# A factorization-machine kernel: four embeddings at a time, 512 moving columns in every product, outer products in two passes of 128 rows, sums in place

## The chip, the core and the metric

The kernel runs on one core of a Trainium2 chip. The metric is device time in microseconds (us), the median of several runs. The core's engines each run a queue of their own, in order: TensorE (PE; its weight loads are shown as PEld), VectorE (DVE), ScalarE (ACT), GpSimd (POOL) and SyncE (SP), which only issues transfers here. Transfers that POOL issues can add to what lies at their destination; transfers that SP issues copy. All of them share 16 DMA engines.

## The reference

```python
out_lin = x @ lin_w.T + lin_b                               # x (1024, 512)
xv = jnp.einsum('bf,efm->bem', x, weight)                   # weight (64, 512, 512)
zp = jnp.einsum('bf,efm->bem', jnp.square(x), jnp.square(weight))
interaction = 0.5 * jnp.sum(jnp.square(xv) - zp, axis=1)
return out_lin + interaction
```

All is float32. For each of 64 embeddings e, x is multiplied by a 512 x 512 matrix, the result is squared, and the squares are summed over e. The sum of zp over e is one product, x squared times the sum of the squared matrices, and is done once at the end.

## The kernel before

The products are made by a two-level block algorithm that needs seven products in place of eight at each level (numbered 1 to 7 at both). The outer level splits the rows of x in two (r), the features in two (kk), and the right side by embedding: a step q takes two embeddings (v), so its four weight blocks are (kk, v). The inner level splits each of those products in the same way. The seven by seven sums of x blocks are kept in `xs`; the sums of weight blocks are made anew for each q by POOL: `outer_t` (L341) makes the outer sums 5, 6, 7 and 4 as tiles `to`, 1,024 elements a partition, and `inner_t` (L373) makes the inner sums 5, 7, 6 and 4 of each outer operand as a tile `ti` (three operations through `sums_t`, L361). `ti` and `to` have three buffers each, the weights four, `z` (results) six, `w2` two.

`block_product` (L403) does one outer product: seven inner products, each by `product` (L389), which multiplies two row halves j of 128 rows by the same 256 moving columns, into the two halves of one PSUM bank. A product in float32 is two instructions on TensorE. Three PSUM tags, x, v and y, hold the partial results: ACT copies x to y after product 1 (L457), then 6, 7 and 4 are added into y, so product 6 waits for ACT's copy. DVE takes results out, with the outer level's sums (`SUMS`, L518): z1, z2, z3, z4, z5 and the four result blocks c11, c12, z5 (which becomes the third) and c21. For outer product 7 POOL adds a part (L446).

`squares` (L476) has ACT square a result block of 2,048 elements a partition in place, and POOL issue one accumulating transfer of 1 MB that adds it to `acc[0]` or `acc[1]`. `w_squares` (L497) squares a weight matrix into a `w2` tile and adds that to `w2_sum` in the same way. A transfer into the same accumulator waits, on POOL, until the one before has landed.

The order is written out by hand: `st.at(t, fn)` gives each piece of work a place t in a stream, and `Stream.run` (L23) emits everything sorted by t. One unit of t is one product (four instructions) in the main loop. Outer products start 7 apart and overlap: at times 0, 2, 4, 6 stand products 1, 5, 6, 2 of one, and between them 7, 3, 4 of the one before. So a step q of two embeddings is 49 units, and there are 32. The stream time fixes only the order in each queue; waits between engines do the rest. SP loads the weights of step q at 49q - 48.8 in transfers of 1 MB.

After the loop the last product (L625 to L749) uses `w2_sum` and the squares of x, and joins the accumulators and the linear part; that linear part is computed at the start (L185 to L300).

Of the kernel before, what the change touches and what calls it, by code (L numbers as in the profile page):

```python
# [28 lines left out]
def kernel(  # L29
# [29 lines left out]

    nc = tc.nc  # L60
# [8 lines left out]
    wpool = ctx.enter_context(tc.tile_pool(name="wpool", bufs=4))  # L69
    topool = ctx.enter_context(tc.tile_pool(name="topool", bufs=3))  # L70
    tipool = ctx.enter_context(tc.tile_pool(name="tipool", bufs=3))
    w2pool = ctx.enter_context(tc.tile_pool(name="w2pool", bufs=2))
    spool = ctx.enter_context(tc.tile_pool(name="spool", bufs=3))
    zpool = ctx.enter_context(tc.tile_pool(name="zpool", bufs=6))
# [7 lines left out]
    w2_sum = const.tile([P, NK, M], F32, tag="w2_sum", name="w2_sum")  # L82
    acc = [
        const.tile([P, 4, BK], F32, tag=f"acc{r}", name=f"acc{r}") for r in range(2)
    ]

# [7 lines left out]
    raw_sb = zpool.tile([P, 7, Q], F32, tag="z", name="raw_sb")  # L94
    a21_sb = w2pool.tile([P, 4, Q], F32, tag="w2", name="a21_sb")
    lw_sb = wpool.tile([P, NK, M], F32, tag="w", name="lw_sb")
# [74 lines left out]
    A21_SUMS = zpool.tile([P, 4, Q], F32, tag="z", name="A21_sums")  # L171
    lt_sb = zpool.tile([P, 2, 4, HM], F32, tag="z", name="lt_sb")
    LT = [lt_sb[:, kk] for kk in range(2)]
# [31 lines left out]
    def lin_out(n):  # L205
        s, j = n // 2, n % 2
        nc.scalar.activation(
            acc[0][:, 2 * s : 2 * s + 2, ts(j, HM)],
            LIN[n].rearrange("p (u c) -> p u c", u=2),
            AF.Copy,  # L210
            scale=2.0,
        )
# [28 lines left out]
    def lin_p(o, bank, first):  # L241
        def fn():
            if o == "1":
                for n in "xvy":
                    LIN[n] = psum.tile(
                        [P, BK], F32, tag=n, name=f"{n}_lin", bufs=2 if n == "x" else 3
                    )
                for n in ("s5", "s2"):
                    LIN[n] = spool.tile([P, BK], F32, tag=n, name=f"{n}_lin")
            for kk in range(2):  # L250
                for j in range(2):
                    nc.tensor.matmul(  # L252
                        LIN[bank][:, ts(j, HM)],
                        lin_x(kk, o)[:, ts(j, P)],
                        operand_b(lw_sb[:, ts(kk, 2)], LT[kk], o),
                        start=(first and kk == 0 and j == 0),
                        stop=True,
                        skip_group_check=True,
                    )

        return fn

    def twice(bank, dst):
        def fn():
            o = LIN[dst] if dst in ("s5", "s2") else acc[1][:, dst]
            nc.scalar.activation(o, LIN[bank], AF.Copy, scale=2.0)
# [3 lines left out]
    def lin_join(bank, s, blk):  # L270
        def fn():
            nc.vector.scalar_tensor_tensor(
                acc[1][:, blk], LIN[bank], 2.0, LIN[s], ALU.mult, ALU.add
# [5 lines left out]
    for kk in range(2):  # L279
        st.at(-30 + 8 * kk, lambda kk=kk: lin(kk))  # L280
        st.at(-30 + kk, lambda kk=kk: sums_t(LT[kk], lw_sb[:, ts(kk, 2)]))
# [22 lines left out]
    def add_bias(r, b):  # L304
        o = acc[r][:, b].rearrange("p (j c) -> p j c", j=2)
        nc.vector.scalar_tensor_tensor(
            o,
            bias[:, ts(b % 2, HM)].unsqueeze(1).broadcast_to([P, 2, HM]),
            2.0,
            o,  # L310
            ALU.mult,
            ALU.add,
        )

    st.at(-1, lambda: nc.sync.dma_start(bias, lin_b.partition_broadcast(P)))


    for b in range(4):
        for r, t in enumerate((23.6, 25.6)):
            st.at(49 * (b + 1) + t, lambda r=r, b=b: add_bias(r, b))  # L320

    W = {}

    def load_w(q):
        for v in range(2):
            W[q, v] = wpool.tile([P, NK, M], F32, tag="w", name=f"w{q}_{v}")
        src = [weight[2 * q + v].rearrange("(p k) m -> p k m", k=NK) for v in range(2)]
        if q == 0:
            for kk in range(2):
                for v in range(2):  # L330
                    nc.sync.dma_start(W[q, v][:, ts(kk, 2)], src[v][:, ts(kk, 2)])
        else:
            for v in range(2):
                nc.sync.dma_start(W[q, v], src[v])

    def w_block(q, kk, v):
        return W[q, v][:, 2 * kk : 2 * kk + 2, :]

    TO = {}

    def outer_t(q, i):  # L341
        B11, B12 = w_block(q, 0, 0), w_block(q, 0, 1)
        B21, B22 = w_block(q, 1, 0), w_block(q, 1, 1)
        t = topool.tile([P, 2, M], F32, tag="to", name=f"to{q}_{i}")
        TO[q, i] = t
        a, b = {
            "5": lambda: (B12, B11),
            "6": lambda: (B22, TO[q, "5"]),
            "7": lambda: (B22, B12),
            "4": lambda: (B21, TO[q, "6"]),  # L350
        }[i]()
        nc.gpsimd.tensor_sub(t, a, b)  # L352

    def outer_b(q, i):
        if i in "123":
            return w_block(q, *{"1": (0, 0), "2": (1, 0), "3": (1, 1)}[i])
        return TO[q, i]
# [3 lines left out]
    def sums_t(t, b):  # L361

        nc.gpsimd.tensor_sub(  # L363
            t[:, 0:2, :],
            b[:, :, HM:M],
            b.rearrange("p l m -> p (l m)")[:, 0:M].rearrange(
                "p (u c) -> p u c", u=2
            ),
        )
        nc.gpsimd.tensor_sub(t[:, 2, :], b[:, 1, HM:M], t[:, 0, :])  # L370
        nc.gpsimd.tensor_sub(t[:, 3, :], b[:, 1, 0:HM], t[:, 2, :])

    def inner_t(q, i):  # L373
        TI[q, i] = tipool.tile([P, 4, HM], F32, tag="ti", name=f"ti{q}_{i}")
        sums_t(TI[q, i], outer_b(q, i))

    def operand_b(b, t, o):
        return {
            "1": lambda: b[:, 0, 0:HM],
            "2": lambda: b[:, 1, 0:HM],  # L380
            "3": lambda: b[:, 1, HM:M],
            "5": lambda: t[:, 0, :],
            "7": lambda: t[:, 1, :],
            "6": lambda: t[:, 2, :],
            "4": lambda: t[:, 3, :],
        }[o]()


    def product(ps, q, i, o, start):  # L389
        rhs = operand_b(outer_b(q, i), TI[q, i], o)  # L390
        for j in range(2):
            nc.tensor.matmul(  # L392
                ps[:, ts(j, HM)],
                xsl(i, o)[:, ts(j, P)],
                rhs,
                start=(start and j == 0),
                stop=True,
                skip_group_check=True,
            )

    Z = {}

    def block_product(t0, q, i, sums):  # L403
# [3 lines left out]
        (addend, name), *more = sums  # L407
        d = {}

        def p(o, bank, start):  # L410
            def fn():
                product(d[bank], q, i, o, start)
# [3 lines left out]
        def p1():  # L416
            for n in "xvy":
                d[n] = psum.tile(
                    [P, BK], F32, tag=n, name=f"{n}{q}_{i}", bufs=2 if n == "x" else 3
                )  # L420
            for n in ("s5", "s2"):
                d[n] = spool.tile([P, BK], F32, tag=n, name=f"{n}_{q}_{i}")
            for n in (name, *(m[1] for m in more)):
                if (q, n) not in Z:
                    Z[q, n] = zpool.tile([P, 4, BK], F32, tag="z", name=f"z{q}_{n}")
            p("1", "x", True)()

        def out_of(bank, dst, blk):
            def fn():
                if addend is None and dst is not None:  # L430
                    nc.scalar.copy(d[dst], d[bank])
                elif addend is None and not more:
                    nc.scalar.copy(Z[q, name][:, blk], d[bank])
                elif addend is not None:
                    o = Z[q, name][:, blk] if dst is None else d[dst]
                    nc.vector.tensor_add(o, d[bank], Z[q, addend][:, blk])  # L436
                for a, n, _ in more if dst is None else ():
                    nc.vector.tensor_add(Z[q, n][:, blk], d[bank], Z[q, a][:, blk])
# [3 lines left out]
        def rest(engine, blk):  # L442
            def fn():
                for _, n, by in more:
                    z = [Z[q, m][:, blk] for m in (n, name, by)]
                    engine.tensor_add(*z)  # L446
# [3 lines left out]
        def join(bank, s, blk):  # L450
            def fn():
                nc.vector.tensor_add(Z[q, name][:, blk], d[bank], d[s])  # L452

            return fn

# [3 lines left out]
        st.at(t0 + 2.5, out_of("v", "s5", 3))  # L459
        st.at(t0 + 4, p("6", "y", False))  # L460
        st.at(t0 + 4.5, out_of("y", "s2", 1))
        st.at(t0 + 6, p("2", "x", False))
        st.at(t0 + 6.5, out_of("x", None, 0))
        st.at(t0 + 8, p("7", "y", False))
        st.at(t0 + 8.5, join("y", "s5", 3))
        st.at(t0 + 10, p("3", "v", False))
        st.at(t0 + 10.5, join("v", "s2", 1))
        st.at(t0 + 12, p("4", "y", False))
        st.at(t0 + 12.5, out_of("y", None, 2))
        if i == "5":  # L470
            st.at(t0 + 9.6, rest(nc.vector, 3))
            st.at(t0 + 11.6, rest(nc.vector, 1))
        elif more:
            st.at(t0 + 11.6, rest(nc.gpsimd, slice(1, 4, 2)))

    def squares(t, q, name, r, wait=5):  # L476
        def sq():
            z = Z[q, name]
# [304 lines left out]
```

## Time and profile before

| | |
|---|---|
| median of 3 runs | 1414.64 us (1413.63 to 1414.66) |
| the profiled execution: device time | 1414.79 us |
| the profiled execution: span, first to last instruction | 1413.0 us |
| mean granted TensorE clock | 1.000 |
| first product of the main loop | 31.33 us |
| POOL's accumulating transfers | 190 of 1 MB, 69.3% of 16 DMA engines' span |
| SP's transfers | 17.7% |

A line of the timeline has the start, the duration (of merged instructions: from the first's start to the last's end), the engine, the source line, the operation, output <- input, shapes, the number of merged instructions, and in brackets the idle time before them with what ended it. Matmuls are pipelined, so that the spacing of their starts, not one's duration, is their cost. "DMA to landing" gives least, median and greatest time from issue to landing; a transfer row has its count, its size and the median of that time.

### The profile page before, as it was taken

How to read it: one execution, taken by the hardware profiler on the slowest of the kernel's cores; microseconds unless marked ns; L12 is line 12 of the kernel's file. 1: busy time of each engine (PE TensorE's matmuls, PEld its weight loads, DVE VectorE, ACT ScalarE, POOL GpSimd, SP SyncE). 2: the span in 40 equal slices, each digit the busy share in tenths (PEclk: the TensorE clock that was granted, in tenths of full speed). 3: DMA queues.
4: the chain of work that ended last, by engine and by line, in shares of the span. 5: the costliest groups of instructions: out<-in, count | busy, mean ns of one | idle time of the engine just before them, and what ended most of it. 6: DMA issues, size and time to landing. Idle time of an engine off the chain costs nothing.

```text
span 1413.0 us, 18120 instructions
## 1 busy us (share of the span) xinstructions
PE 1408.7 (100%) x6476; PEld 1231.0 (87%) x6476; DVE 918.9 (65%) x1339; ACT 617.9 (44%) x824; POOL 1181.6 (84%) x1047
## 2 busy tenths in 40 slices
PE   9999999999999999999999999999999999999999
PEld 6888888888888888888888888888888888888887
DVE  5766667665666765666765666765666765666664
ACT  2345444445444445444345444345444345444353
POOL 6888988888988888888888888888888888888884
PEclk9999999999999999999999999999999999999999
DMA  5499888889888889988889998889988899998884
GB/s 216 92 200 211 201 201 199 189 196 211 200 199 199 191 194 210 202 201 198 193 193 207 205 201 198 195 191 203 208 199 199 198 189 200 208 202 198 200 176 119
DMA packets 41161, 275.11 MB, mean 195 GB/s; under 512 B 4464, under 2 KB 7024, under 8 KB 8560
## 3 DMA queue, kind: packets, MB, share of 16 engines
q0 software_dynamic: 27360, 199.24, 69.3%
q1 hardware_dynamic: 13424, 74.19, 17.7%
q8 instruction: 52, 0.85, 0.2%
q10 hardware_dynamic: 288, 0.52, 0.1%
q14 instruction: 37, 0.30, 0.1%
HBM read 72.61 MB, written 2.10 MB: 53 GB/s over the span
## 4 chain that ended last, share of the span: by engine, by line
PE 100%; DVE 0%; issue 0%
PE y L392 41%; PE v L392 27%; PE x L392 27%; PE lin L197 1%; PE y_last L628 1%; PE x_last L628 0%; PE v_last L628 0%; PE y_lin L252 0%; PE y_spin L183 0%; PE x_lin L252 0%; PE v_lin L252 0%; PE end L691 0%; DVE o_last L701 0%
## 5 line engine op out<-in xcount | busy, mean ns | idle before, releaser
L392 PE MATMUL y<-ti,xs 128*128 128x256 f32 x2688 | 653.5, 379 | 0.0
L392 PEld LDWEIGHTS y<-ti,xs 128*128 128x128 f32 x2688 | 510.6, 190 | 69.7 <-issue 0.3
L457 ACT COPY y<-x 128x512 f32<-128x512 f32 x224 | 127.7, 570 | 618.7 <-PE x L392 613.2
L392 PE MATMUL x<-to,xs 128*128 128x256 f32 x1024 | 252.3, 379 | 0.0
L392 PE MATMUL v<-ti,xs 128*128 128x256 f32 x896 | 229.9, 379 | 0.0
L392 PEld LDWEIGHTS x<-to,xs 128*128 128x128 f32 x1024 | 194.6, 190 | 26.5
L363 POOL TENSOR_TENSOR ti<-to 128x512 f32<-128x512 f32 x128 | 180.9, 1413 | 32.7 <-PE y L392 29.3
L352 POOL TENSOR_TENSOR to<-w,to 128x1024 f32<-128x1024 f32 x64 | 158.4, 2474 | 44.2 <-PE v L392 44.2
L481 ACT ACTIVATE z_c<-z_c 128x1024 f32<-128x1024 f32 x192 | 192.6, 1053 | 0.0
L392 PE MATMUL x<-w,xs 128*128 128x256 f32 x768 | 191.9, 379 | 0.0
L392 PEld LDWEIGHTS v<-ti,xs 128*128 128x128 f32 x896 | 170.2, 190 | 23.1
L452 DVE TENSOR_TENSOR z_z<-y,s 128x512 f32<-128x512 f32 x128 | 88.0, 687 | 125.7 <-PE y L392 125.7
L392 PEld LDWEIGHTS x<-w,xs 128*128 128x128 f32 x768 | 145.9, 190 | 19.8
L363 POOL TENSOR_TENSOR ti<-w 128x512 f32<-128x512 f32 x96 | 131.3, 1368 | 19.6 <-PE y L392 19.6
L392 PE MATMUL v<-to,xs 128*128 128x256 f32 x512 | 131.4, 379 | 0.0
L494 POOL DMA_DIRECT2D acc<-z_c x95 | 83.1, 874 | 55.0 <-ACT z_c L481 47.1
L436 DVE TENSOR_TENSOR s<-y,z_z 128x512 f32<-128x512 f32 x160 | 110.3, 689 | 28.4 <-PE y L392 22.7
L506 ACT ACTIVATE w<-w 128x1024 f32<-128x1024 f32 x126 | 126.3, 1054 | 0.0
L452 DVE TENSOR_TENSOR z_c<-y,s 128x512 f32<-128x512 f32 x96 | 66.4, 692 | 89.2 <-PE y L392 89.2
L436 DVE TENSOR_TENSOR s<-v,z_z 128x512 f32<-128x512 f32 x160 | 110.1, 688 | 17.9 <-PE v L392 11.0
L452 DVE TENSOR_TENSOR z_z<-v,s 128x512 f32<-128x512 f32 x128 | 87.7, 685 | 36.1 <-PE v L392 36.1
L392 PEld LDWEIGHTS v<-to,xs 128*128 128x128 f32 x512 | 97.3, 190 | 13.2
(122 smaller groups left out, 1623.2 us busy)
## 6 DMA issues: line engine op xcount, KB each, us to landing
acc<-z_c POOLq DMA_DIRECT2D x95, 1024.0 KB, 7.6
w_sum<-w POOLq DMA_DIRECT2D x63, 1024.0 KB, 8.4
w<-weight SPq DMA_DIRECT2D x62, 1024.0 KB, 6.2
acc<-z_z POOLq DMA_DIRECT2D x32, 1024.0 KB, 7.8
w<-weight SPq DMA_DIRECT2D x4, 512.0 KB, 8.1
xq<-x SPq DMA_DIRECT2D x2, 1024.0 KB, 5.7
out<-o_last SPq DMA_DIRECT2D x7, 256.0 KB, 2.3
xs<-x SPq DMA_DIRECT2D x2, 384.0 KB, 7.5
```

Source lines behind the costliest of these rows:

```text
L197: nc.tensor.matmul(LIN[n], quarter(0, kk, (0, 1, 3, 2)[2 * s + l])[:, ts(j, P)], lw_sb[:, 2 * kk + l, :], start=(kk == 0 and l == 0), stop ...
L352: nc.gpsimd.tensor_sub(t, a, b)
L363: nc.gpsimd.tensor_sub(t[:, 0:2, :], b[:, :, HM:M], b.rearrange("p l m -> p (l m)")[:, 0:M].rearrange("p (u c) -> p u c", u=2),)
L392: nc.tensor.matmul(ps[:, ts(j, HM)], xsl(i, o)[:, ts(j, P)], rhs, start=(start and j == 0), stop=True, skip_group_check=True,)
L436: nc.vector.tensor_add(o, d[bank], Z[q, addend][:, blk])
L452: nc.vector.tensor_add(Z[q, name][:, blk], d[bank], d[s])
L457: st.at(t0 + 0.5, lambda: nc.scalar.copy(d["y"], d["x"]))
L481: nc.scalar.activation(o, o, AF.Square)
L494: lambda: nc.gpsimd.dma_start(acc[r], Z[q, name], accum_op=ALU.add),
L506: nc.scalar.activation(w2[:, ts(h, 2)], W[q, v][:, ts(h, 2)], AF.Square)
L628: nc.tensor.matmul(ps[:, ts(j, HM)], last_x(i)[:, (0, 1, 3, 2)[2 * s + l], ts(j, P)], last_w(i)[:, l, :], start=(start and j == 0 and l == 0),
```

## The change

A step q now takes four embeddings: v picks a pair, and each block is (kk, v) with both embeddings u of the pair beside each other. The moving operand of an inner product is 512 columns, 256 of either embedding, and each outer product runs as two passes (`unit`) of seven inner products, pass j with 128 rows of each block. There are 16 steps of 98 stream units. One unit of t is again one product, now of two instructions.

The buffers are fixed: four weight blocks `WB`, the outer sums in T5 and T6 and, for 7, in the place of block (0, 0); the inner sums in three tags of two buffers each (`tp` holds 5 and 7); three result tiles `ZT`, where a, b and c are the sums of the outer level, made in place, and a and c change places with every step; and one tile `w2_sb` for the squares of weights. Each result tile is added to its accumulator by two transfers of 1 MB, one for each embedding of a pair (`gather`). For outer product 5 POOL adds a part in each pass (`rest_dst`). The outer x sums for 3 move from POOL to DVE. At the end, the last c21 is added by DVE, and POOL adds the two halves of the last a before one transfer.

The core of the diff:

```diff
+    def outer_t(i):
...
+        for u in range(2):
+            nc.gpsimd.tensor_sub(OUTER[i][:, u], a[:, u], b[:, u])
...
+        t = TI[q, i] = {
+            n: tpool.tile([P, k, M], F32, tag=n, name=f"{n}_{q}_{i}")
+            for n, k in (("tp", 2), ("t6", 1), ("t4", 1))
+        }
+        nc.gpsimd.tensor_sub(t["tp"], b[:, 1], b[:, :, 0])
+        nc.gpsimd.tensor_sub(t["t6"][:, 0], b[:, 1, 1], t["tp"][:, 0])
+        nc.gpsimd.tensor_sub(t["t4"][:, 0], b[:, 0, 1], t["t6"][:, 0])
...
+                nc.tensor.matmul(
+                    d[bank],
+                    xsl(i, o)[:, ts(j, P)],
+                    operand_b(q, i, o),
...
+    def gather(t, q, n, r, u):
         st.at(
             t,
+            lambda: nc.gpsimd.dma_start(acc[r], place(q, n)[:, u], accum_op=ALU.add),
+        )
...
+        def sq(kk):
+            o = (w2_sum if first else w2_sb)[:, ts(kk, 2)]
+            nc.scalar.activation(o, WB[kk][v][:, u], AF.Square)
...
+                t + 3.5,
+                lambda: nc.gpsimd.dma_start(w2_sum, w2_sb, accum_op=ALU.add),
...
+    UNITS = {
+        "1": (None, "a"),
+        "2": ("a", "c"),
+        "6": ("a", "a"),
+        "7": ("a", "b"),
+        "5": ("b", "c"),
+        "3": ("a", "a"),
+        "4": ("b", "b"),
     }
-    NQ = E // 2
+    NQ = E // 4
     for q in range(NQ):
-        g0 = 49 * q
...
+        g0 = 98 * q
+        last = q == NQ - 1
+        for kk, v, t in ((1, 0, -41), (0, 1, -39), (0, 0, -37), (1, 1, -10)):
+            if q:
+                st.at(g0 + t, lambda q=q, kk=kk, v=v: load_w(q, kk, v))
+        for i, t in (("5", -19 if q else -8), ("6", 8.5), ("7", 22.5), ("4", 50.5)):
+            st.at(g0 + t, lambda i=i: outer_t(i))
+        for n, (i, (addend, dst)) in enumerate(UNITS.items()):
+            st.at(g0 + 14 * n - 11.5, lambda q=q, i=i: inner_t(q, i))
+            for j in range(2):
+                unit(g0 + 14 * n + 7 * j, q, i, j, addend, dst)
+
+        for t0, n, r in ((21, "c", 0), (63, "c", 1), (77, "a", 0), (91, "b", 1)):
+            for j in range(2):
+                t = t0 + 7 * j + 7.6 + (3 if n == "c" and r else 0)
...
+            for u in range(2):
+                gather(g0 + t0 + 18 + 10 * u, q, n, r, u)
+        if q == 0:
+            w_times = (1, 4, 30, 56)
+        else:
+            w_times = (-16, 0, 30, 56)
+        for n, t in enumerate(w_times):
+            w_squares(g0 + t, q, n // 2, n % 2)
```

## The prediction

> **What bounds the kernel now.** I read the page's first part, its chain of waits, then the timelines by engine.
>
> ```profile
> PE 1408.7 (100%) x6476; PEld 1231.0 (87%) x6476; DVE 918.9 (65%) x1339; ACT 617.9 (44%) x824; POOL 1181.6 (84%) x1047
> PE 100%; DVE 0%; issue 0%
> ```
>
> TensorE is busy from end to end and the chain never leaves it. So time comes only from fewer nanoseconds per product, and every wait that reaches TensorE is paid in full. POOL, at 84%, has the least room of the others.
>
> The TensorE timeline gives the price of both widths, since the linear part already has 512 columns:
>
> ```profile
> 8.94 7.03 PE L197 MATMUL lin<-lw_sb,xs 128*128 128x512 f32 x16
> 15.81 1.02 PE L197 MATMUL lin<-lw_sb,raw_sb 128*128 128x512 f32 x2
> ...
> 1388.61 1.89 PE L628 MATMUL y_last<-tw,sx 128*128 128x256 f32 x8
> ...
> 1407.61 1.89 PE L691 MATMUL end<-tw,xq 128*128 128x256 f32 x8
> ```
>
> Sixteen wide instructions take 15.81 - 8.94 = 6.87 us, 0.4292 each; from 1388.61 to 1407.61 there are 88 narrow ones, 0.2159 each. A product of 256 columns over two row halves is four narrow instructions, 0.8636; the new product of 512 columns and 128 rows is two wide ones, 0.8583, which I call a slot.
>
> The POOL and DMA rows price what decides below:
>
> ```profile
> 618.66 2.36 POOL L352 TENSOR_TENSOR to<-w,w 128x1024 f32<-128x1024 f32 x1
> 620.97 0.85 POOL L494 DMA_DIRECT2D acc<-z_z  x1
> 621.58 1.55 POOL L363 TENSOR_TENSOR ti<-w 128x512 f32<-128x512 f32 x1
> ...
> DMA to landing us min/median/max: 7.0/7.8/8.6
> ...
> w_sum<-w POOLq DMA_DIRECT2D x1, 1024.0 KB, 11.4
> w<-weight SPq DMA_DIRECT2D x1, 1024.0 KB, 6.5
> ```
>
> A 1,024-element POOL operation costs 2.31 from start to start. The landing row is of two accumulating transfers issued at 627.0 and 631.0: the first lands 7.0 later, the second, queued behind it, 8.6 later, so 5.6 after the first. The last two rows are an accumulation and a weight load issued together: the accumulation needs 11.4, where w_sum accumulations issued alone need 7.5.
>
> **What goes: narrow products.** 6,272 narrow instructions become 3,136 wide ones: 6,272 x 0.2159 - 3,136 x 0.4292 = 1354.1 - 1346.0 = 8.1; the starts of the whole main loop (31.33 to 1388.61, with sixteen other narrow instructions) give 0.2158 and 7.8. I take 7.8. Weight loads halve; at 190 ns each behind a 429 ns product they cost nothing either way.
>
> **What stays.** For four embeddings DVE still does 80 operations of 0.69 and ACT the same copies and squares. POOL's inner sums go from 14 x (1.26 + 0.72 + 0.73 with gaps, 2.83) = 39.6 to 7 x 5.0 = 35.0 (2.36 + 1.26 + 1.26 with gaps); nothing, as POOL isn't the chain. Accumulations stay at twelve of 1 MB. Weight loads come in runs of 4 KB; issued three together some 18 slots ahead of use, they are hidden. Head and tail move by work that other work hides; I allow 3 us either way.
>
> **What is added: waits in the order of POOL, ACT and the accumulation queue.** Before, the twelve accumulations are spread, and w2 alternates between two buffers. Now eight of twelve fall between stream times 81 and 119, 38 slots or 32.6 us, where eight at 5.35 need 42.8. The two halves of each result add to the same accumulator, so the second waits on POOL, in order, until the first has landed; and `w2_sb` is one buffer, so ACT's next square waits for its accumulation.
>
> I follow one quad from slot 72 (zero), with a the time at which POOL starts the inner sums of product 4. They wait for slot 71, the last reader of their buffer (two in place of three); POOL rows start 0.26 after such a slot ends (590.03 to 590.29), so a is at least 0.26. Prices: inner sums 5.0, each outer operation 2.31, POOL's part of product 5 2.33, an issue 0.95. A transfer on an empty queue lands after 7.4 (rows 7.0 to 7.85), one queued 5.35 after the one ahead (5.0 to 5.75; the queue's 69.3% of the span over 190 transfers is 5.15).
>
> Inner 4 ends at a + 5.0, POOL's part of 5 at a + 7.33, outer 5 (two operations) at a + 11.95. Then the first half of c is issued and at a + 12.9 w2. The half lands at a + 19.35. The load of the fourth weight block waits for slot 87 and is issued at 14.0, about together with them. How far it delays them mid-queue no row shows: between 0.6 (the accumulation at 620.97, 2.2 after a load, took 8.06) and 3.9 (11.4 - 7.5, issued together). I take 3.9, the nearer. w2 lands at a + 19.35 + 5.35 + 3.9 = a + 28.6.
>
> ACT's square of the second embedding, placed at the quad's time 0, waits for that. Behind it on ACT stands the copy of x to y, and TensorE's product 6 at slot 102 waits for the copy. Squares 1.9, copy 0.57, two hand-overs of 0.15: a + 31.4. Slot 102 is due at 30 x 0.8583 = 25.75. TensorE stands for a + 5.6.
>
> The queue goes on: c second half lands at a + 33.95, a first half 39.3, w2 44.65, a second half 50.0, b first half 55.35 (a to be added). DVE's join of product 2 overwrites what "a second half" reads; behind it wait DVE's sums, and slot 124 needs it at 44.6 + a + 5.6 = a + 50.2, it can have it at a + 51.0: another 0.8.
>
> POOL meanwhile: the second half of a can't be issued before a + 39.3; outer 6, b's first half, inner 6 to a + 50.8; b's second half waits to a + 55.35; outer 7 and inner 7 to a + 65.95; w2 and the next c (queued: it lands 12.75 after w2's issue, a + 78.7); inner 5; the second half of c waits to a + 78.7; outer 4, inner 3, w2, POOL's part of 5: a + 92.5. That is when the next inner 4 starts. POOL's round is 92.5 us against TensorE's 98 x 0.8583 = 84.1: 8.4 a quad. TensorE's own waits, a + 5.6 + 0.8, reach 8.4 at a = 2.0, where both agree. POOL's other sums come before TensorE needs them (outer 7 at 62.9, slot 140 at 58.3 + 8.4).
>
> Fifteen boundaries: the first at a = 0.26, 6.7; fourteen at 8.4, 117.6; together 124.3. Span 1413.0 - 7.8 + 124.3 = 1529.5. The median 1414.64 lies 1.64 above the span: **1531**.
>
> All ends low (7.0, 5.0, 0.6): the round is 86.0 and the stall 1.9, 15 x 1.9 = 28, hence 1435. All high (7.85, 5.75, 3.9): a round of 96.3, 183 in all, 1590. These make the range.
>
> **Where the skill differs.** The Trainium skill, "DMA: Bandwidth & Descriptors", Anatomy of one DMA, gives a POOL-issued transfer 2.0 us plus its bytes over 436 GB/s, 4.4 for 1 MB; the accumulations here need 7.0 to 7.85. By the page w2 would be down some 6 us earlier and slot 102 unhindered, which would give the saving alone, 1407; the row decides. The same skill, "TensorE: Matmul & The Clock Gate", What's actually happening, halves TensorE's clock after an idle window of about 3.4 us until some 3.4 us of work have passed; by it each stall of 7.6 us would be followed by about 1.7 us lost, 15 x 1.7 = 25 more, 1556 (an estimate from that page).
>
> **Rivals.** First, faster: the accumulations keep up, and only the narrow instructions go: 1414.6 - 7.8 = 1407. The place is ACT's wait for w2 at the quad's start; it is free if w2 lands by 25.75 - 2.8 = 22.95. For: POOL would be 84% busy at most. Against: from a + 12.9 that leaves 9.8 us for a transfer queued behind another, while 0.26 + 11.95 + 7.0 + 5.0 is 24.2 with no load in the way at all. 0.12; within 0.2%, 0.03.
>
> Second, only ACT's wait bites: transfers at the quick end let POOL catch up (round 86 to 88), TensorE loses 2 to 4 a quad: 1435 to 1470. For: the queue's mean of 5.15. Against: the 11.4 landing. 0.25.
>
> Third, a slow clock on top. At the start of the trace wide instructions run at half rate; these rows
>
> ```profile
> 0.78 3.75 PE L183 MATMUL y_spin<-const-float32-0.0 128*128 128x512 f32 x4 [0.78 <-PEq L772]
> 4.54 2.84 PE L197 MATMUL lin<-lw_sb,xs 128*128 128x512 f32 x4
> ```
>
> show four in 3.76 us against 1.72 later; full rate comes about 5.6 us after the first, a loss of 2.8. A stall of 7.6 may bring it back each time. POOL's round absorbs a's 1.74 and the 0.8, so 0.3 a quad is left, 5 us; if cold stretches also fall on smaller stalls, 2.8 a quad, 42: 1536 to 1573. Against: no row shows TensorE idle that long after its start. 0.10.
>
> That the change doesn't do what it says is excluded: the built program has 1,568 products of 512 columns there.
>
> **How the numbers follow.** A measurement of this kernel can tell about 0.2% (3 us). Forecast 0.50 (its own range 1480 to 1575), quick transfers 0.25, cold clock 0.10, faster 0.12, same 0.03. Faster 0.12, same 0.03, slower 0.85. Low is the low bound, 1435; the upper end 1575 leaves out the last part of the high bound, together with the faster cases under 2 in 10.
>
> **What would show it.** Right: wide instructions at 0.429; TensorE's only long idle times once a quad, at a y product whose copy ACT made late, and the y copy waiting behind squares of w; POOL standing before second halves for 4 to 8 us; w2 landing 14 to 16 us after its issue; quads of 91 to 93 us. Wrong: w2 landing under 10 us; stalls at other products (then a buffer or weight load I called hidden); or a chain that stays on TensorE throughout.

## The result and the profile after

The changed kernel takes 1557.65 us (median of 6 runs, 1555.19 to 1561.9); the kernel before, on the same chip, 1414.7 us. The ratio is 1.101, with a 95% interval of 1.0998 to 1.1031: slower by a tenth. The profiled execution has a span of 1557.8 us, 144.8 more than before.

The page's first part (busy time, share of the span and instructions of each engine), its chain of waits, and two of its costliest groups; in a group, the part behind the bar is the busy time, the mean ns of one, and the engine's idle time before them with what ended most of it:

```profile
PE 1442.4 (93%) x3340; PEld 647.4 (42%) x3340; DVE 950.7 (61%) x1347; ACT 622.5 (40%) x824; POOL 1135.9 (73%) x705
PE 47%; DMA 34%; POOL 11%; issue 5%; DVE 2%; ACT 2%; SPq 0%; POOLq 0%; ACTq 0%; DVEq 0%
L420 PE MATMUL y<-t,xs 128*128 128x512 f32 x896 | 448.5, 625 | 102.7 <-ACT y L480 99.8
L519 ACT ACTIVATE w_sb<-w 128x1024 f32<-128x1024 f32 x126 | 125.9, 1048 | 153.5 <-DMA w_sum<-w_sb 152.6
```

TensorE has half the instructions, as the change says, and is no longer the whole chain: a third of it is transfers. A step q of four embeddings is called a quad here, a half of c, a or b is the part that one `gather` adds, and w2 stands for the squares of weights in `w2_sb`. Busy time is no sign of saved work here, since instructions at the slow clock count as busy too. The two groups name one wait: products into the y bank stood 99.8 us for ACT's copy of x to y, and ACT's squares of w stood 152.6 us for the accumulation of w2. The list of waits (engine and line, what for, total us, times, longest) gives the count:

```profile
POOL acc L511 <- DMA acc<-z: 216.1, 59, 6.2
ACT w_sb L519 <- DMA w_sum<-w_sb: 152.6, 20, 11.2
PE y L420 <- ACT y L480: 99.8, 15, 7.8
```

Fifteen waits, one at each boundary between quads. This is the timeline around one of them, by engine:

```profile
1061.92 1.02 PE L420 MATMUL v<-t,xs 128*128 128x512 f32 x2
1070.12 3.52 PE L420 MATMUL y<-t,xs 128*128 128x512 f32 x4 [7.17 <-ACT y L480]
1073.47 1.88 PE L420 MATMUL x<-w,xs 128*128 128x512 f32 x4
...
1067.49 2.00 ACT L519 ACTIVATE w_sb<-w 128x1024 f32<-128x1024 f32 x2 [10.60 <-DMA w_sum<-w_sb]
1069.40 0.58 ACT L480 COPY y<-x 128x512 f32<-128x512 f32 x1
...
1051.63 0.86 POOL L511 DMA_DIRECT2D acc<-z  x1
1052.21 1.17 POOL L526 DMA_DIRECT2D w_sum<-w_sb  x1
1062.80 1.77 POOL L511 DMA_DIRECT2D acc<-z  x2 [4.34 <-DMA acc<-z]
```

Read it from below. POOL issues w2 at 1052.21, behind the first half of c; by the transfer's record it lands at 1067.41, 15.20 later. ACT, in order, can then square the next w (1067.49), and only then copy x to y (1069.40). TensorE, which had work until 1062.9, starts again at 1070.12. The next four instructions take 3.35 us to the start of the following ones, 0.84 each in place of 0.43: the granted clock is at 0.5 there, and at every one of the fifteen waits, for 3.4 to 10.2 us that begin within the wait (at the first of them, 0.7 us behind it).

From one quad to the next it is 93.39 us on average, 98 slots being 84.1. The start lost time too: the first product of the main loop starts at 36.76 in place of 31.33. The timeline shows why, on TensorE and on DVE; the last line is the same join in the kernel before:

```profile
33.19 2.08 PE L271 MATMUL y_lin<-z,z 128*128 128x256 f32 x4 [4.14 <-DVE acc L309]
36.76 1.92 PE L420 MATMUL x<-w,xs 128*128 128x512 f32 x2
...
14.68 0.41 DVE L252 TENSOR_TENSOR z<-z 128x256 f32<-128x256 f32 x1
23.59 2.57 DVE L181 TENSOR_TENSOR xs<-z,xs 128x256 f32<-128x256 f32 x1
28.58 2.56 DVE L183 TENSOR_TENSOR xs<-xs,z 128x256 f32<-128x256 f32 x1
32.46 0.68 DVE L309 SCALAR_TENSOR_TENSOR acc<-y_lin,s_lin 128x512 f32<-128x512 f32 x1
...
28.15 0.69 DVE L272 SCALAR_TENSOR_TENSOR acc<-y_lin,s_lin 128x512 f32<-128x512 f32 x1 [7.51 <-PE y_lin L252]
```

The change moves the x sums of 6 ahead of the linear part's first join, where only those of 5 stood. DVE makes such a sum in 0.41 us at best, but in up to 2.57 while POOL makes its weight sums, and the join that TensorE waits for stands behind them (32.46 in place of 28.15).

The sum, from the starts of TensorE's instructions: wide products -7.9 (0.4292 against twice 0.21585, the mean over the whole loop before, 3,136 times), the later start +5.4, waits in the loop +108.1, slow products behind waits +39.5: 145.1, for 144.8 measured.

### The profile page after: what moved, and what is told of

Its sections match the earlier page's. It is cut to its first block, busy times and chain, and to the rows that moved or that the text cites. A ratio compares the mean times of both kernels' runs of the same rounds, so it can differ in the third digit from the quotient of the medians.

```text
span 1557.8 us, 11107 instructions
## 1 busy us (share of the span) xinstructions
PE 1442.4 (93%) x3340; PEld 647.4 (42%) x3340; DVE 950.7 (61%) x1347; ACT 622.5 (40%) x824; POOL 1135.9 (73%) x705
## 3 DMA queue, kind: packets, MB, share of 16 engines
q1 hardware_dynamic: 21328, 74.19, 15.5%
## 4 chain that ended last, share of the span: by engine, by line
PE 47%; DMA 34%; POOL 11%; issue 5%; DVE 2%; ACT 2%; SPq 0%; POOLq 0%; ACTq 0%; DVEq 0%
PE y L420 20%; PE x L420 13%; DMA w<-weight 12%; DMA w_sum<-w_sb 12%; PE v L420 11%; DMA acc<-z 10%; POOL t L381 5%; POOL tp L392 2%; POOL w L381 1%; ACT w_sb L519 1%; POOL t L393 1%; POOL acc L511 1%; POOL z L475 1%; DVE xs L182 1%; PE y_last L643 1%
## 5 line engine op out<-in xcount | busy, mean ns | idle before, releaser
L420 PE MATMUL y<-t,xs 128*128 128x512 f32 x896 | 448.5, 625 | 102.7 <-ACT y L480 99.8
L420 PEld LDWEIGHTS y<-t,xs 128*128 128x128 f32 x896 | 176.2, 199 | 329.8 <-issue 320.1
L511 POOL DMA_DIRECT2D acc<-z x125 | 118.8, 985 | 225.8 <-DMA acc<-z 216.1
L466 DVE TENSOR_TENSOR z<-y,s 128x512 f32<-128x512 f32 x192 | 132.6, 690 | 243.6 <-PE y L420 242.0
L503 ACT ACTIVATE z<-z 128x1024 f32<-128x1024 f32 x256 | 258.9, 1053 | 39.4 <-POOL z L475 22.2
L420 PE MATMUL x<-w,xs 128*128 128x512 f32 x512 | 257.5, 611 | 0.0
L420 PE MATMUL y<-tp,xs 128*128 128x512 f32 x448 | 229.5, 594 | 4.7 <-DVE s L445 2.9
L420 PE MATMUL v<-tp,xs 128*128 128x512 f32 x448 | 229.1, 593 | 0.0
L420 PE MATMUL x<-t,xs 128*128 128x512 f32 x384 | 188.3, 592 | 0.0
L519 ACT ACTIVATE w_sb<-w 128x1024 f32<-128x1024 f32 x126 | 125.9, 1048 | 153.5 <-DMA w_sum<-w_sb 152.6
L392 POOL TENSOR_TENSOR tp<-w 128x1024 f32<-128x1024 f32 x64 | 172.4, 2693 | 7.8 <-PE y L420 6.5
L381 POOL TENSOR_TENSOR t<-w,t 128x1024 f32<-128x1024 f32 x64 | 158.9, 2656 | 0.0
```

The costliest lines, as they stand in the source:

```text
L381: nc.gpsimd.tensor_sub(OUTER[i][:, u], a[:, u], b[:, u])
L392: nc.gpsimd.tensor_sub(t["tp"], b[:, 1], b[:, :, 0])
L420: nc.tensor.matmul(d[bank], xsl(i, o)[:, ts(j, P)], operand_b(q, i, o), start=start, stop=True, skip_group_check=True,)
L466: nc.vector.tensor_add(s if both else zblk(q, dst, j, b), d[bank], s)
L503: lambda u=u: nc.scalar.activation(z[:, u, j], z[:, u, j], AF.Square),
L511: lambda: nc.gpsimd.dma_start(acc[r], place(q, n)[:, u], accum_op=ALU.add),
```

## The experiments

Twelve kernels, all made from the changed one. Each is given with the median of its own runs; the kernel before took 1414.1 to 1414.6 beside them.

**1. Without the accumulations of c, a and b** (all quads but the last; those terms are missing from the output).

```diff
-                gather(g0 + t0 + 18 + 10 * u, q, n, r, u)
+                if last:
+                    gather(g0 + t0 + 18 + 10 * u, q, n, r, u)
```

> The changed kernel without the accumulations of squared results (c, a and b) of all quads but the last; it leaves those terms out of the output. The accumulations of w2 stay. Theory (all of the loss in the main loop comes from waits that start at the accumulation queue, and the products of 512 columns themselves cost what the rows say): no stall at the boundaries, 1414.6 - 7.8 and some 5 to 14 us of the head (its first product starts 5.4 us later and stands three times): 1412 to 1421. Rival (POOL's tensor work or DVE is a limit of its own in the new arrangement): 1430 or more.

Measured: 1417.23 (ratio 1.0026, 1.0015 to 1.0036). Its chain, and how long POOL's transfers of w2 take (count, size, us to landing):

```profile
PE 96%; DVE 2%; issue 1%; ACT 0%; DMA 0%; SPq 0%; DVEq 0%
...
w_sum<-w_sb POOLq DMA_DIRECT2D x63, 1024.0 KB, 7.1
```

From the second quad on, each takes 84.12 us. So all that the main loop loses behind its start hangs on the accumulations, and none of it on wide products, POOL's sums or DVE by themselves. The main loop, with the 7.1 of waits and slow products of its start taken off, is 1342.86 against 1351.02 before: the wide products save 8.2. What is left above that is the start.

**2. The squares of w later.** Three of a quad's four squares of w move back in ACT's order. Their transfers follow them, 3.5 slots behind, so POOL's order changes too: the second accumulation of w2 goes from slot 3.5 to 15.5, the third from 33.5 to 44.5, the fourth by one.

```diff
-            w_times = (-16, 0, 30, 56)
+            w_times = (-16, 12, 41, 57)
```

> The changed kernel with ACT's order alone moved: the squares of w for the second, third and fourth embedding of a quad stand at its slots 12, 41 and 57 in place of 0, 30 and 56, so that the copy of x to y of product 1 no longer stands behind a square that waits for w2's accumulation. Theory (ACT's in-order wait is what stops TensorE): the 7.2 us stall and the 2.3 us of half clock behind it go at all 15 boundaries; the next thing late is the second half of a, which landed 24.7 us (29 slots) after the quad's start and whose place product 2 overwrites from slots 20 to 22, so a smaller stall of 0 to 4 us can be left there: 1430 to 1480. Rival (POOL's and the accumulation queue's round of 92.5 us is the limit, ACT is only where it shows): the stall moves to another product, 1530 to 1558.

Measured: 1482.35 (1.0485, 1.0469 to 1.0501), quads of 88.8. Its waits:

```profile
DVE z L466 <- DMA acc<-z: 124.3, 29, 7.3
ACT w_sb L519 <- DMA w_sum<-w_sb: 10.8, 14, 1.8
PE y L420 <- DVE z L466: 35.2, 16, 3.7
POOL acc L511 <- DMA acc<-z: 147.4, 45, 10.1
```

ACT's wait is gone and 75 us with it, half of the loss: with the copies ahead of the square that waits, TensorE no longer stands at product 6. But the run does not part ACT's order from POOL's. POOL stood 147.4 us for accumulations in place of 216.1, and it started the inner sums of product 4 at the earliest moment that TensorE allowed in all sixteen quads, in place of nine; so the moved transfers shortened POOL's round as well. The time is just past the range of the theory, and another wait is left than it named: DVE's join of product 1 now stands for the second half of c, whose place it overwrites (landed 1026.44, the join at 1026.56, TensorE's wait of 3.71 ended 1027.40), not for the second half of a.

**3. The fourth weight block's load later.**

```diff
-        for kk, v, t in ((1, 0, -41), (0, 1, -39), (0, 0, -37), (1, 1, -10)):
-            if q:
+        for kk, v, t in ((1, 0, -41), (0, 1, -39), (0, 0, -37), (1, 1, 1)):
+            if q and (kk, v) == (1, 1):
+                st.at(g0 + t, lambda q=q: load_w(q, 1, 1, nc.scalar))
+            elif q:
```

> The changed kernel with the load of the fourth weight block of each quad given to ACT behind the first product's y copy (slot 1) in place of SP at slot 87, so that it no longer runs beside the first half of c and w2. My prediction put the load's delay at 3.9 us of w2's landing, out of bounds 0.6 to 3.9. Theory (3.9): w2 lands 11 to 12 us after its issue in place of 15.2, the stall falls from 7.2 to 3.3 and the half clock behind it to at most 2.3: 1557 less 15 x 3.9 = 58, so 1495 to 1505 (down to 1470 if the shorter stall leaves the clock alone). Rival (0.6, the accumulations take that long in a queue of two anyway): 1545 to 1555. If outer 6, which needs that block, comes late now, a stall at a product of 6 shows and the time says nothing on it.

Measured: 1555.55 (1.0998, 1.0976 to 1.102), quads of 93.0. TensorE's waits, then three lines of the timeline:

```profile
PE y L420 <- ACT y L480: 50.1, 15, 4.7
PE y L420 <- DVE s L445: 20.3, 14, 2.5
PE y L420 <- DVE z L466: 18.6, 11, 3.2
...
1032.84 2.64 POOL L392 TENSOR_TENSOR tp<-t 128x1024 f32<-128x1024 f32 x1
1046.84 1.17 POOL L526 DMA_DIRECT2D w_sum<-w_sb  x1
1032.34 3.69 DVE L472 TENSOR_TENSOR z<-z,s 128x512 f32<-128x512 f32 x1
```

The mechanism is as expected: w2 lands 11.58 after its issue in place of 15.20, so the load costs it 3.6, and the waits for ACT are halved. The time stays nearly the same. The load now delays the first half of a (17.64 to landing, 13.85 in the changed kernel) and with it POOL: the inner sums of product 4 start without any wait, 1.5 us later against TensorE's slot 72 than in the changed kernel (mean over fourteen quads), so POOL is what is late. Its inner sums now run beside DVE's sums of L472 and these are slow (3.69 for one of 0.68; 107 us for the 64 of them, 73 in the changed kernel), and two new waits of TensorE take what ACT's gave back. So with this place of the load a second limit lies at 93.0 a quad, 0.4 under the first.

**4. Products in the idle time.** Twelve products into the y bank at each boundary, ahead of the copy that overwrites it:

```diff
+        def warm():
+            for _ in range(12):
+                nc.tensor.matmul(d["y"], xsl(i, "1")[:, ts(j, P)], operand_b(q, i, "1"),
...
+        if q and i == "1" and j == 0:
+            st.at(t0 + 0.4, warm)
```

> The changed kernel with twelve products of 512 columns (5.2 us) added at each of the 15 boundaries, into the y bank that the late copy then overwrites: they run in the time in which TensorE stood. The stall's end, set by ACT, stays where it is. Theory (the slow products behind the stall are the clock, brought down by the idle time): they run at 0.43 us, and 2.3 x 15 = 34 us less 2 to 6 us for what is left of the clock's loss and for boundaries whose stall was shorter than the added work: 1525 to 1532. Rival (the products after the stall are slow for another reason, reads of SBUF beside the transfers, say): 1555 to 1562.

Measured: 1582.97 (1.1182, 1.1163 to 1.12), a miss of the edit, not of the theory. The timeline shows twice the work that was meant:

```profile
1079.09 10.46 PE L482 MATMUL y<-w,xs 128*128 128x512 f32 x24
```

A product is two instructions, so 10.3 us were added where 9.3 were to be had. It shows one thing all the same: from the second quad on the clock is at full speed, and quads of 95.0 are 84.1, the 10.3 added and 0.6 more, so next to nothing else is late.

**5. The same with six products** (`range(6)`).

> As the run with added products, but with six of them at each boundary: a product of 512 columns is two instructions, so twelve were 10.3 us, more than the stall; six are 5.15. The 15 added groups fill most of a stall whose end is set by ACT. Theory (the slow products behind the stall are the clock): the half clock behind the boundaries goes, 15 x 2.3 = 34 us, less 2 to 10 for boundaries with a stall under 5.15 us and for what ring takes the place of the clock's loss (the round of POOL and the accumulations was 92.5 against 93.98 measured, which leaves at most 1.5 x 15 = 22 to gain): 1528 to 1545. Rival (another reason for the slow products): 1555 to 1562 with the 36 us of slow products still there.

Measured: 1551.41 (1.0976, 1.0961 to 1.0991); quads of 93.2. TensorE's waits:

```profile
PE y L420 <- ACT y L493: 25.4, 11, 3.0
PE y L420 <- DVE s L445: 10.5, 12, 2.2
```

The mean granted clock rises from 0.962 to 0.989, and what slow instructions cost (starts spaced by more than the full-speed price, with no idle time between) falls from 40.8 us to 21.4 over the span. But the time falls by 6 only, well short of the 12 to 30 expected. Two things took the rest: waits for DVE's sums grew from 2.9 us to 10.5, and the copies came later still, with POOL starting the inner sums of 4 on average 1.4 us behind slot 72, in place of 0.7. That this is the limit of run 3 is likely from the quads (93.0 and 93.2), but not shown. The rival of another cause for the slow products is out, since the same products run at 0.43 where TensorE hadn't stood.

**6. The first two accumulations of w2 moved**, with outer 7 and the third squares moved behind them.

```diff
-            w_times = (-16, 0, 30, 56)
+            w_times = ((-16, 10.9), (28.7, 32.2), (42, 45.5), (56, 59.5))
...
-("7", 22.5)
+("7", 29.5)
```

(squares and transfer of each embedding; a list of outer sums in the last two lines)

> The changed kernel with w2's first two accumulations alone moved: the first from before the boundary to slot 10.9, behind c and a and ahead of b, the second from 3.5 to 32.2 with its squares at 28.7 (outer 7 and the third squares follow to 29.5 and 42); c, a and b, the loads and the start stay. Theory (w2 stands in the queue between the halves of c and is what ACT and c's second half wait for): c's second half lands 5 us earlier, in time for product 1, and the boundary stalls are under 1 us: 1420 to 1440. Rival (c behind outer 5, or the load beside it, are enough to stop TensorE): 1460 to 1500.

Measured: 1643.11 (1.1616, 1.1595 to 1.1638), the slowest of all. Its timeline within one quad:

```profile
860.56 0.87 POOL L526 DMA_DIRECT2D w_sum<-w_sb  x1
...
867.59 2.00 ACT L519 ACTIVATE w_sb<-w 128x1024 f32<-128x1024 f32 x2 [15.27 <-issue]
...
870.23 3.44 PE L420 MATMUL y<-t,xs 128*128 128x512 f32 x4 [10.26 <-ACT y L480]
```

The boundary (near 820 in this quad) is free of waits, as the theory had it. But I put the third squares at slot 42, ahead of a copy of x to y, and POOL came to issue the second accumulation only at 860.56, held by the second half of b and the sums behind it. It landed at 867.52; TensorE stood 10.26 us. Quads take 99.1 us: the same mechanism at another slot costs more than the one removed.

**7. All twelve accumulations spread.**

```diff
+    GATHER = {("c", 0): (39, 51), ("c", 1): (81, 86.4),
+              ("a", 0): (95, 106.6), ("b", 1): (110.1, 127.9)}
-        ... ("5", -19 if q else -8), ("6", 8.5), ("7", 22.5), ("4", 50.5)
+        ... ("5", -16.5 if q else -8), ("6", 3.2 if q else 8.5), ("7", 24.5), ("4", 50.5)
-            w_times = (-16, 0, 30, 56)
+            w_times = ((-16, 12), (24, 27.5), (46, 49.5), (61.5, 65))
```

(inner 2 goes from 2.5 to 9.5, two weight loads change places, a bias goes from 36.6 to 48.6)

> The changed kernel with the twelve accumulations of a quad spread anew in the stream, and with nothing else taken out: c's first half before outer 5 and its second half right behind it, a's halves ahead of b's, w2's first accumulation from before the boundary to slot 12, its second from 3.5 to 27.5, and the squares of w, the sums that stand beside them (outer 5, 6, 7, inner 2) and two loads moved to suit. Theory (the products are quick and only the order of accumulations stopped TensorE): no stall at the boundaries, the time of the kernel without c, a and b accumulations (1417) within 5: 1412 to 1422. Rival (twelve accumulations a quad at 5.35 to 6.2 us each, delayed by four loads, are too much for 84.1 us however they are ordered): 1440 or more, with stalls behind whichever accumulation is late.

Measured: 1419.33 (1.0036, 1.0023 to 1.0048); quads of 84.7. As expected: the queue carries all twelve in time. All but 5 us of what the changed kernel lost, it lost to the order alone.

**8 to 12. Towards a kernel that beats both.** The start's sums moved (and the first quad's squares of w, to slots 18 and 22):

```diff
-        (inner_x("5"), -7),
-        (outer_x("7") + inner_x("7"), 1.6),
+        (outer_x("7"), -3.4),
+        (inner_x("5", nc.gpsimd) + inner_x("7", nc.gpsimd) + outer_x("3", nc.gpsimd), 12),
+        (inner_x("3", nc.gpsimd), 31),
```

> The run with the spread accumulations, and the sums of x of the start moved as well: inner 5 and 7, outer 3 and inner 3 go to POOL at slots 12 and 31, outer 7 behind the linear part's last join, and the first quad's squares of w to slots 18 and 22, so that DVE's join isn't late for TensorE. Theory (12 us of the start are these waits: 8.8 of idle time and the clock behind it): 1404 to 1411, the 1414.6 less 7.8 that wide products were worth, so faster than before by 0.3 to 0.7%. Rival (the start's loss only moves, into POOL's sums of the first quad): 1412 to 1422.

Measured: 1414.88 (1.0005, 0.9996 to 1.0014). The start's loss is gone (the loop starts at 30.73, no wait in it), but 8.0 us of waits under 0.7 us are left in the loop. The next kernel went for these:

```diff
-        ("c", 0): (39, 51),
+        ("c", 0): (39, 48),
-        for kk, v, t in ((1, 0, -41), (0, 0, -38), (0, 1, -36), (1, 1, -10)):
+        for kk, v, t in ((1, 0, -41), (0, 0, -38), (0, 1, -24.6), (1, 1, -10)):
-            w_times = ((-16, 12), (24, 27.5), (46, 49.5), (61.5, 65))
+            w_times = ((-3.5, 12), (24, 27.5), (46, 51), (73.2, 76.7))
```

> The run with the spread accumulations and the moved start, with one more wait taken away. Its trace leaves 8.0 us of waits under 0.7 us in the main loop: POOL's part of product 5 stands 5.3 to 6.4 us for the second half of the other c, which lands 13 us after its issue beside three loads, and with it POOL's inner sums of product 4 and ACT's squares of c are late. Here that half is issued at slot 48, right behind the first and ahead of w2's third accumulation (51) and of the loads, w2's fourth goes to 76.7 with its squares at 73.2, the second weight block's load follows them, and the next quad's first squares of w stand at -3.5. Theory: POOL no longer stands there and the 8 us go: 1405 to 1409, 0.4 to 0.7% under the kernel before. Rival (the accumulations delay something else by as much): 1412 to 1418.

Measured: 1461.22 (1.0327, 1.0313 to 1.0341). A miss: w2's fourth accumulation now stood ahead of c's first half, which landed 13.0 after its issue; POOL stood 7.7 for it with inner 1 behind, and TensorE waited for inner sums. So inner 1 and inner 2 were put ahead of what POOL waits for:

```diff
-        ("c", 1): (81, 86.4),
+        ("c", 1): (81, 91),
-            st.at(g0 + (9.5 if q and n == 1 else 14 * n - 11.5), ...
+            st.at(g0 + (3 if q and n == 1 else 14 * n - 11.5), ...
```

> The last re-spread kernel (1461) with POOL's order changed in two places: inner 1 stands ahead of c's second half, and inner 2 ahead of outer 6 and of a's second half. In its trace 29 waits of 0.9 to 2.3 us at products 5 of units 1 and 2, 46 us in all, were for POOL's inner sums, which stood behind those halves for 7.7 and 1.9 us; the copies that ACT makes and the waits behind c are short there. Theory: those waits go and nothing takes their place: 1405 to 1411, under the kernel before by 0.3 to 0.7%. Rival (the first halves then come too late for the joins that overwrite c and a): 1420 to 1460.

Measured: 1420.88 (1.0044, 1.0031 to 1.0058). The waits for inner sums are gone; 15.7 us are left by the spacing of starts, of which 8.8 are waits for copies (11 times), which stand behind squares of w. So, with outer 7 later as well:

```diff
-                t = t0 + 7 * j + 7.6 + (3 if n == "c" and r else 0)
+                t = t0 + 7 * j + 7.6 + (7 - 4 * j if n == "c" and r else 0)
-            w_times = ((-3.5, 12), (24, 27.5), (46, 51), (73.2, 76.7))
+            w_times = ((-3.5, 12), (28.55, 28.8), (46, 51), (73.2, 76.7))
```

> The last kernel (1421) with ACT's order changed in two places: the squares of w of the second embedding stand behind the y copy of slot 28.5 and not before it, and c's squares of the first row half behind the y copy of slot 77.5. In its trace 15.7 us of waits of 0.5 to 1.4 us are left at y products, whose copy stood behind squares of w that waited 3.5 to 6.5 us for w2. Theory: these go, and the start has no wait any more, so the time is 1414.6 less the wide products' 8: 1404 to 1410, 0.3 to 0.7% under the kernel before. Rival (outer 7 or c's first half, now later, take their place): 1412 to 1425.

Measured: 1415.52 (1.0008, 0.9999 to 1.0017), with 4.3 of the 9.3 us that are left in one place of the last quad: a wait of 2.5 and the half clock behind it. The last step:

```diff
-        for r, t in enumerate((22.6, 48.6)):
+        for r, t in enumerate((36.6, 48.6)):
-    for t, r, kk in ((-26, 1, 0), (-25, 1, 1), (-22, 0, 0), (-21, 0, 1)):
+    for t, r, kk in ((-26, 1, 0), (-25, 1, 1), (-19.9, 0, 0), (-19.8, 0, 1)):
```

> The last kernel (1415.5) with its two largest left waits moved: the squares of the last stage's x, second part, from slot -22 to -19.9 of the tail (behind the y copy, which stood 5.6 us for that load: 5.5 us with the clock behind it), and the bias of the first accumulator from slot 22.6 to 36.6 (2.2 us in four quads at products whose sums stand behind it). Theory: 1413.7 - 7.7 = 1406 for the span's own run, 1405 to 1410 for the median, under the kernel before by 0.3 to 0.6%. Rival (scattered waits of other accumulations, which change from run to run, weigh as much): 1411 to 1416.

Measured: 1411.07 (1408.26 to 1415.42 in 11 runs; ratio 0.9982, 0.9972 to 0.9991). Its page, first part and chain, and its waits:

```profile
PE 1403.3 (100%) x3340; PEld 633.3 (45%) x3340; DVE 927.4 (66%) x1333; ACT 621.1 (44%) x824; POOL 1151.7 (82%) x719
PE 81%; DMA 12%; POOL 3%; issue 2%; DVE 1%; ACT 1%; POOLq 0%; ACTq 0%; DVEq 0%
```

```profile
PE y L420 <- DVE z L466: 1.1, 4, 0.4
PE y L420 <- DVE s L445: 0.6, 2, 0.3
PE y L420 <- ACT y L480: 0.5, 1, 0.5
```

This is the first version under the kernel before, by 0.2%, 147 us under the change as it was made. Its waits in the loop (2.2 us by the list, 5.7 by the spacing of starts) fall in other places in other quads. Its runs spread over 7 us, against 1.4 for the kernel before, as the rival's waits that change from run to run would have it; no run shows that they are the reason.

## Why the prediction came out as it did

**The saving.** Forecast 7.8; 7.9 by the durations, 8.2 by the loop of run 1. Right.

**The place.** TensorE's one long wait a quad is at a product 6 whose copy ACT made late, behind a square that waits for w2. Right. Run 2 takes this wait away, and half of the loss goes; how much of that is ACT's order and how much POOL's, which the same edit changed, no run parts.

**w2's landing.** Forecast 5.35 behind the first half of c plus 3.9 for the load, which is 15.7 after the issue; measured 15.20, and 11.58 without the load, so 3.6 for it. Right. The Trainium skill, "DMA: Bandwidth & Descriptors", Anatomy of one DMA, would have 4.4 for a lone transfer (an estimate from its fit); w2's accumulations landed after 7.1 (median) in run 1, where the loop has no other accumulations. The row was the right choice.

**The stall's size.** Forecast 7.6 from a = 2.0; 7.17 in the boundary shown, though a was at its earliest, where my own sum gives 5.9. The missing 1.3 has two terms. The greater was put at nothing: "issued three together some 18 slots ahead of use, they are hidden". They were not, in eleven places:

```profile
POOL t L381 <- DMA w<-weight: 12.7, 11, 1.6
...
1046.99 4.70 POOL L381 TENSOR_TENSOR t<-w,w 128x1024 f32<-128x1024 f32 x2 [1.42 <-DMA w<-weight]
```

POOL stood 1.42 us for one of the three loads before outer 5, and the third landed 16.91 after its issue, beside an accumulation. The other term was sized too low: the inner sums of 4 took 5.9 (1037.28 to 1043.20), not 5.0. With 0.4 saved at the issues, w2 was issued 2.0 later than the sum has it, at 1052.21; its landing, 0.5 quicker than the sum's, and smaller terms gave 0.7 back.

**What sets the quad.** Forecast: POOL's round, 92.5, so 8.4 lost. Measured 93.39, so 9.27, and POOL's round was not what held it in most: in nine of sixteen quads POOL started the inner sums of 4 at the earliest moment that TensorE allowed, and a was 0.67 on average, not 2.0. TensorE's own loss (on average 6.8 of wait and 2.2 of half clock a boundary) came first. The round seems to lie close behind: the two runs that shortened TensorE's loss and left w2's place in POOL's order (3 and 5) ended at 93.0 and 93.2, near the 92.5 of the sum, and the one that also moved w2's transfers (2) went to 88.8. So the two limits were probably sized about right and their order was wrong; no run removes POOL's alone. That 8.4 came so near 9.27 is in part luck: the sum has 1.7 of a late a and 0.8 at slot 124, where the run has 2.2 of half clock and the later w2.

**The clock.** I gave it a rival of its own, with the argument that POOL's round would absorb it. The half clock came at all fifteen boundaries, 2.2 a quad, and the measured time lies in that rival's range (1536 to 1573); by run 5 taking about half of the clock's loss away was worth 6 us in all. So the argument held for the time, in that another limit took the gain, though what the changed kernel paid was the clock. The Trainium skill, "TensorE: Matmul & The Clock Gate", What's actually happening, has the half clock after an idle window of about 3.4 us, and 1.7 was my estimate of the loss from it. The waits of 4.5 to 7.9 here agree with the first, and lost more than the estimate. In run 2, from the second quad on, six of the seven waits of 2.7 us and over (by the spacing of starts) came with half clock, one of 2.37 too, and none of the shorter ones, so a wait under the page's window can be enough.

**Head and tail.** "I allow 3 us either way": measured 12.4, by run 1 (its span of 1417.2 against 1413.0 less the 8.2 saved). This is the term I failed to work out: the move of the x sums stood in the diff, and the prediction costed no instruction of it. (Run 8 takes the start's loss away, by moving those sums and the first quad's squares of w together.) With 15 x 9.27 = 139.1 in place of 124.3 for the quads (14.8) it makes 27.2, for the 26.7 us between 1531 and 1557.65.

**The rivals.** "The accumulations keep up" did not come true as the order was written; run 7 shows that they can. "Only ACT's wait bites" did not either: its 2 to 4 a quad assumed quick transfers. The 0.8 at slot 124 was not seen as such; all waits for DVE's sums in the loop come to 5.8 us, 2.9 of it in the first quad.

## What to carry to other kernels

When buffers are merged, draw one period of the transfer queue with its landings against the first instruction that overwrites each source, and mark every in-order engine that waits for a landing: what stands behind that wait, not the wait itself, is the price. Before removing the wait that shows, work out the next limit; here most of what two experiments removed (3 and 5) came back at once, moving three squares and their transfers was worth 75 us, and the order as a whole 138. And cost every instruction that moves in the diff's start, too, however small. When an experiment moves one engine's work, look for what moves with it on another.

## What the runs showed of the hardware

- Accumulations within SBUF land 7.0 us after the issue for 1 MB with nothing ahead (changed kernel, issued at 1103.44), 11.4 when issued with another ahead (1104.02), 15.2 with a weight load beside as well (1052.21). Three plain loads of 1 MB, issued within 1.1 us of 1028.92, landed after 5.6, 10.0 and 16.9, the last beside an accumulation of w2.
- DVE sums with both inputs in SBUF grow from 0.41 to 2.57 us (256 elements, changed kernel) and from 0.68 to 3.69 (512, run 3) beside POOL's sums: in the changed kernel the 15 of 256 elements and the 15 of 512 that ran with no sum of POOL beside them took at most 0.43 and 0.69. Those that read PSUM stay at 0.69 through the loop, with POOL busy 73% of the time.
- At half clock a wide instruction takes 0.853 us for 0.429. It lasts 3.4 to 10.2 us by the clock records of the changed kernel, in steps of 3.4, and at fourteen of fifteen boundaries the end of the wait that brought it on is part of that time.
